# A four-image conv-attention and expert network on one core: the last attention block's sums move into its projection, and the end is re-ordered

## The chip, the cores and the metric

The kernel runs on one core of one Trainium2 chip, in one launch. The metric is the device time of that launch in microseconds (us). The core has a matrix engine (TensorE, "PE" in the profile; its weight loads are "PEld"), VectorE ("DVE"), ScalarE ("ACT"), GpSimd ("POOL") and SyncE ("SP"), which here only issues transfers. Sixteen DMA engines move data between HBM and the on-chip memory SBUF. TensorE writes to a second on-chip memory, PSUM, from which VectorE and ScalarE read.

## The reference: what is computed

The input x has 4 images of 128 channels and 64 x 64 = 4096 positions. Two layers follow each other, all in float32.

```python
# layer 0, per image (gn: group norm over groups of 4 channels)
e1, e2, asm = prelu(w1 @ gn(x)), prelu(w2 @ gn(x)), prelu(wa @ gn(x))   # 64, 64, 128 channels
x = x + softmax(e1.T @ e2) @ asm            # 4096 x 4096 scores
# layer 1, tokens t = x.T, per image (ln: layer norm over the 128 channels)
t = t + softmax((ln(t) @ Wq.T) @ (ln(t) @ Wk.T).T / 128) @ (ln(t) @ Wv.T)
logits = ln(t) @ gate_w.T + gate_b          # 64 experts
probs  = softmax(logits, axis=tokens)       # each expert picks its 8 best tokens
pooled = sum over those 8 of prob * ln(t)   # one vector for each image and expert
out_e  = gelu([pooled, 1] @ weight1[e]) -> [h, 1] @ weight2[e]   # 129x512, 513x128
t[token] += out_e * prob                    # given back to the 8 tokens
```

The two attentions are nearly all of the arithmetic. The experts are nearly all of the weights: 64 experts of 0.5 MB.

## The kernel before, in words

**Attention stages.** `stage(b, layer, ...)` runs the attention of one image and layer, in eight blocks n of 512 queries. `attention` (L523) makes the scores of four 128-key chunks at a time (L542, two PSUM tiles `ps`), ScalarE takes the exponential (L551), and `products` (L458) adds the product with the values into the PSUM tile `av`. The eight stages follow each other (L1082 to L1092); norms, projections and routing of other images are generators that are stepped beside them. The order within each engine is the order in which the Python code emits instructions, except where a scheduler moves one; `keep_in_program_order` pins an instruction, and `no_sync_barrier` lets no instruction move across it.

**Seven products.** In layer 1 the value product is a 2 x 2 block scheme with seven products instead of eight. `mix` (L483) makes the needed differences of two exponential tiles on VectorE, `mixed_products` (L495) adds seven products into the four quarters of `av[:, 0:2, 0:512]` (two halves of 64 partitions, two PSUM banks, two halves of 256 queries). The quarters have still to be added up to get the block's 128 x 512 result. `finish_attn` (L615) does that: ScalarE copies `av` to `c0`, `c1` and the half-swapped `sw` (L626 to L630), VectorE makes the sums `u` with six additions (L633 to L638). Then `u` is multiplied by `wvd`, the value weights with a 129th column that gives the softmax denominator (L647, `pv`); a reciprocal, a multiply-add with the residual `xq` and a copy of the denominator follow (L653 to L660).

**The last block.** For image 3, block 7 (`final`), no attention stage follows, so this chain is exposed: `xT` -> layer norm `norm_tokens` (L336; the power is taken on POOL, L181) -> transposes (`x_c` for the residual, stored to `x2` by ACT at L670; `l` at L678) -> `tg` -> gate product `pg` (L710) -> `M` -> `last_route` (L868): best eight, exponentials, the selection `zl` (L916), its transposes `pzT` (L923), `pool` (L928, L932) -> `pooledT`.

**Experts.** 16 groups g of 4 experts: `first_product` (L1124, `ph`, copied to `hp` by VectorE), `hidden` (L1134: transposes `pht`, bias add `hT`, GELU), `second_product` (L1147, `po`), each one group behind the one before. A group's weights are 2 MB, loaded by SP in two 1 MB halves (`load`, L1039). Nine places hold them: groups 0 to 8 go to places 0 to 8, group g + 9 to the place of group g, its first half after g's first product and its second half after g's second product. Groups 2, 6, 7 come early; groups 0, 1 go into the keys' and values' tiles `t`, `tt` as the last stage lets them go, 3 to 5 into `ring` when the attention's pool is released (L1103), group 8 into `late_place`, where the routing's tiles (pool `blk`) were (L1110 to L1117).

**Scores and checks.** `last_scores` (L936) is stepped in the expert loop at g = 11 (`half_g + 3`): VectorE's MATCH_REPLACE over 64 x 4096 (its line is L768), and after the loop ScalarE's exponentials and POOL's subtractions. At the same g `watch` (L1699) reduces the recorded softmax sums on VectorE, multiplies with ones on TensorE (L1720) and stores a count; after everything, a branch takes a general kernel if a sum was out of bounds (L1725).

**The end.** `first_pair` (the probabilities of images 0 and 1) is loaded into place 7 (L1194); the residual `x2` of two images and half of the positions is loaded into each of the places 0 to 3, one DMA an image (L1203). Then, for each pair i and block n, TensorE spreads the expert outputs (L1217, `px`), VectorE adds them to `x2` (L1224) and after every second block ACT issues two stores of 0.5 MB (L1227). The DMAs of SP and ACT share eight semaphores in turn, in the order in which the built program has them: each waits for the DMA eight before it.

Of the kernel before, what the change touches and what calls it, by code (L numbers as in the profile page):

```python
# [9 lines left out]
F32 = mybir.dt.float32  # L10
# [16 lines left out]
def tile_unshifted(  # L27
# [56 lines left out]
    def dram_tile(shape, name):  # L84
        return dram.tile(shape, F32, tag=name, name=name)

    x2 = [dram_tile([P, S], f"x2_{b}") for b in range(B)]
    x2_block = [[dram_tile([P, BLK], f"xb_{b}_{n}") for n in range(NB)] for b in range(B)]  # L90
# [327 lines left out]
    wvd = const.tile([P, C + 1], F32, tag="wvd", name="wvd")  # L418

    def weights_qk():  # L420
        wT = []
        for nm, w in (("q", wqT), ("k", wkT)):
            pw = ms_tile(f"pw{nm}")
            nc.tensor.matmul(pw[:, :P], lhsT=w, rhs=unfold, start=True, stop=True)
            t = block_tile("te", f"w{nm}")[:, :P]
            nc.vector.tensor_copy(t, pw[:, :P])
            wT.append(t)
        yield
        pw = ms_tile("pwqk")
        nc.tensor.matmul(pw[:, :P], lhsT=wT[0], rhs=wT[1], start=True, stop=True)  # L430
        nc.vector.tensor_copy(wqk, pw[:, :P])
        yield
        pw = ms_tile("pwv")
        nc.tensor.matmul(pw[:, :P], lhsT=unfold, rhs=wv, start=True, stop=True)
        nc.vector.tensor_copy(wvd[:, :C], pw[:, :P])
        nc.vector.tensor_copy(wvd[:, C : C + 1], last[:, 0:1])
        yield

# [176 lines left out]
    def finish_attn(b, n):  # L615
# [5 lines left out]

        direct, final = b == B - 1 and n >= NB - 2, b == B - 1 and n == NB - 1
        if final:
            c0, b1 = av[:, 0, :], av[:, 1, :]
        else:
            nc.scalar.copy(c0, av[:, 0, :])  # L626
            nc.scalar.copy(c1, av[:, 1, :])
            b1 = c1
        nc.scalar.copy(sw[lo, :], av[hi, 1, :])
        nc.scalar.copy(sw[hi, :], av[lo, 1, :])  # L630
        one, two = slice(0, HB), slice(HB, BLK)

        nc.vector.tensor_add(c1, b1, sw)  # L633
        nc.vector.tensor_add(u[:, two], c1[:, one], c1[:, two])
        nc.vector.tensor_add(u[:, two], u[:, two], c0[:, one])
        nc.vector.tensor_add(u[:, one], c1[:, two], c0[:, two])
        nc.vector.tensor_add(u[hi, one], u[hi, one], c0[hi, one])
        nc.vector.tensor_add(u[hi, one], u[hi, one], sw[hi, one])  # L638
        yield
# [3 lines left out]
        for k, (s0, ns) in enumerate(((2, 2), (0, 2)) if final else ((0, 3), (3, 1))):  # L643
            pv = ms_tile(f"pv{nm}_{k}")[:, : ns * (C + 1)].rearrange("p (s c) -> p s c", c=C + 1)
            for s in range(ns):
                for h in range(2):
                    nc.tensor.matmul(  # L647
                        pv[bass.ts(h, HC), s, :],
                        lhsT=u[:, (s0 + s) * P + h * HC : (s0 + s) * P + (h + 1) * HC], rhs=wvd,
                        start=True, stop=True,  # L650
                    )
            i = slice((b * NB + n) * SUB + s0, (b * NB + n) * SUB + s0 + ns)
            nc.vector.reciprocal(top_inv[:, i], pv[:, :, C])  # L653
            for s in range(ns):
# [4 lines left out]
                )  # L659
            nc.vector.tensor_copy(top_sum[:, i], pv[:, :, C])  # L660
        yield
        tb = pools["blk"].tile([P, SUB, C], F32, tag="tb", name=f"tb{nm}")
        tg = block_tile("c1", f"tg{nm}")
        if direct:
# [4 lines left out]
            to_channels(xT, xp, f"x2_{b}_{n}")  # L669
            nc.scalar.dma_start(out=x2[b][:, bass.ts(n, BLK)], in_=xp)  # L670
            yield
            if final:
# [68 lines left out]

    def small_tile(tag, b, width, dtype=F32):
        return small.tile([P, width], dtype, tag=tag, name=f"{tag}{b}")

# [93 lines left out]
    def early_route(b):  # L838
# [3 lines left out]
        m = M[b // 2][hs, : S - BLK]  # L842
        top, neg = small_tile("e_top", b, 8), small_tile("e_neg", b, 1)
        at, tot = small_tile("r_at", b, 8, mybir.dt.uint32), small_tile("e_tot", b, NB)
# [120 lines left out]


    def run(gen):
        for _ in gen:
            pass
# [69 lines left out]
    def load(g, i, h):  # L1039
        W[g] = places_of[i]  # L1040
        nc.sync.dma_start(out=W[g][:, h, :], in_=packed[g][:, h, :])
# [3 lines left out]
    def first_weights():  # L1045

        w1b = block_tile("xq", "w1b", 4)[:E, :]
        nc.sync.dma_start(out=w1b, in_=a["weight1"][:, D1 - 1, :])
# [20 lines left out]
    def last_weights(n, g):  # L1069
# [4 lines left out]
        if n == NB - 1:  # L1074
# [18 lines left out]
          ahead=mix_values(3), pace=(2, 1), hook=last_weights)  # L1093
    products()


# [8 lines left out]
    for g in range(3, 6):  # L1105
        new_place(g, ring, "w")
        for h in range(2):
            load(g, g, h)
    last_top = last_route(B - 1, pooledT)
    ends["blk"].close()  # L1110
    late = ctx.enter_context(tc.tile_pool(name="late", bufs=1, side="right", reuse_waits="tile"))
    late_place = late.tile([P, S], F32, tag="z", name="late_place")
    place(8, late_place)
    scores = last_scores(B - 1, *last_top)

    for h in range(2):
# [59 lines left out]
    for g in range(E // EG + 2):  # L1176
# [7 lines left out]
        for half, now in ((0, g), (1, g - 2)):  # L1184
            if 0 <= now and now + 9 < E // EG:
                load(now + 9, now, half)
        if g == half_g + 3:
            next(scores)
            watch(ms_tile("watch")[0:1, 0:1])
    next(scores)  # L1190
# [7 lines left out]
    for i in range(B // 2):  # L1198
        for q in range(2):
            ys.append(places_of[2 * i + q])  # L1200
            for h in range(2):
                tc.keep_in_program_order(
                    nc.sync.dma_start(out=ys[-1][:, h, :], in_=x2[2 * i + h][:, bass.ts(q, HS)])  # L1203
                )
    for i in range(B // 2):
        pe = ms_tile(f"poe{i}")
# [473 lines left out]
def tile_conv_attn_hybrid(ctx: ExitStack, tc: tile.TileContext, a: dict, out: bass.AP):  # L1680
# [17 lines left out]

    def watch(pc):  # L1699
        ok = guard.tile([P, 4], F32, tag="ok", name="ok")  # L1700

        later = tc.keep_in_program_order
        later(nc.vector.tensor_reduce(ok[:, 0:1], all_sum, axis=AX.X, op=ALU.max))
        later(nc.vector.tensor_reduce(ok[:, 1:2], all_inv, axis=AX.X, op=ALU.max))
        nc.vector.tensor_scalar(ok[:, 0:1], ok[:, 0:1], SAFE_SUM, None, op0=ALU.is_le)
        nc.vector.tensor_scalar(ok[:, 1:2], ok[:, 1:2], SAFE_INV, None, op0=ALU.is_le)
        later(nc.vector.tensor_reduce(ok[:, 2:3], top_sum, axis=AX.X, op=ALU.max))
        later(nc.vector.tensor_reduce(ok[:, 3:4], top_inv, axis=AX.X, op=ALU.max))
        nc.vector.tensor_mul(ok[:, 2:3], ok[:, 2:3], ok[:, 3:4])
        nc.vector.tensor_scalar(ok[:, 2:3], ok[:, 2:3], SAFE_RATIO, None, op0=ALU.is_le)  # L1710

        later(nc.vector.tensor_reduce(ok[:, 3:4], top_inv, axis=AX.X, op=ALU.add))
        nc.vector.tensor_scalar(ok[:, 3:4], ok[:, 3:4], SAFE_INV, None, op0=ALU.is_le)
        both = guard.tile([P, 1], F32, tag="both", name="both")
        nc.vector.tensor_mul(both, ok[:, 0:1], ok[:, 1:2])
        nc.vector.tensor_mul(both, both, ok[:, 2:3])
        nc.vector.tensor_mul(both, both, ok[:, 3:4])
        ones = guard.tile([P, 1], F32, tag="ones_g", name="ones_g")
        nc.gpsimd.memset(ones, 1.0)
        nc.tensor.matmul(pc, lhsT=both, rhs=ones, start=True, stop=True)  # L1720
        nc.vector.tensor_copy(count, pc)

# [44 lines left out]
```

## Time and profile before

| what | us |
|---|---|
| median of 3 runs | 3296.14 (3294.93 to 3297.43) |
| the profiled execution | 3298.76 |
| its span in the profile | 3297.0 |
| TensorE busy in the span | 3227.0 (98%) |
| VectorE busy | 2123.0 (64%) |
| ScalarE busy | 1253.4 (38%) |
| GpSimd busy | 424.4 (13%) |
| last value product of the attention ends | 3179.2 |
| first expert product starts | 3202.5 |
| first addition of the end (L1224) starts | 3264.4 |
| last addition of the end starts | 3285.5 |

All times in the profile are counted from the start of its span. The profiled execution is 2.62 us above the median of the runs, and 1.76 us of it lie outside the span. "Busy" for TensorE means that a product was in the pipeline; "granted clock" is the share of TensorE's full clock that it was given. A line such as `PE L542 ... ps<-q,t 128*64 128x512 f32 x4096` names engine, source line, output and input tiles, shape and count; a float32 product is recorded as two instructions. In a line of the timeline, the brackets hold the idle time of the engine before the instruction and what ended it. `w`, `t` and `tt` are names of tiles in the places above; `x` on the right of a DMA is an `x2` tensor, `wp` the packed weights.

### The profile page before, as it was taken

The page shows a single profiled execution, that of the slowest core. Times are in us where ns is not written, and L with a number is a line of the kernel's source. Part 1 is how long each engine was busy: PE and PEld are TensorE (multiplying, and loading weights), DVE is VectorE, ACT ScalarE, POOL GpSimd, SP SyncE. Part 2 cuts the span into 40 slices and gives each one's busy share as a digit, 9 for nine tenths or more (in the row PEclk, how much of TensorE's full clock was granted, in tenths as well). Part 3 has the DMA queues.
Part 4 walks back from the last instruction along what each step waited for, and adds up shares of the span by engine and source line. Part 5 has one row for each costly group of instructions (what it writes and reads, how often), then busy time and mean ns, then how long its engine had stood idle before and what let it go on. Part 6 is the DMA issues. An engine that isn't in the chain of part 4 may idle for free.

```text
span 3297.0 us, 49453 instructions
## 1 busy us (share of the span) xinstructions
PE 3227.0 (98%) x19764; PEld 1602.7 (49%) x19764; DVE 2123.0 (64%) x4192; ACT 1253.4 (38%) x1432; POOL 424.4 (13%) x414
## 2 busy tenths in 40 slices
PE   8999999999999999999999999999999999999986
PEld 4444444445555644444555554444444455454443
DVE  6665567556665667756675657765776566666566
ACT  2333334433333335333433335333333333343432
POOL 0111112310000004241000002242100002010011
PEclk9999999999999999999999999999999999999988
DMA  3221244223323222311120111321231010131059
GB/s 88 52 53 28 56 113 122 74 82 80 90 73 85 55 55 54 70 31 36 39 53 23 39 26 39 91 64 26 45 75 39 20 40 20 33 108 39 17 203 373
DMA packets 364753, 223.31 MB, mean 68 GB/s; under 512 B 273632, under 2 KB 298720, under 8 KB 359136
## 3 DMA queue, kind: packets, MB, share of 16 engines
q1 hardware_dynamic: 359056, 208.54, 23.6%
q10 hardware_dynamic: 4944, 10.46, 0.8%
q8 instruction: 157, 2.57, 0.3%
q0 software_dynamic: 512, 1.05, 0.1%
q14 instruction: 84, 0.69, 0.1%
HBM read 159.75 MB, written 97.19 MB: 78 GB/s over the span
## 4 chain that ended last, share of the span: by engine, by line
PE 96%; DVE 2%; DMA 1%; issue 0%; POOL 0%; ACT 0%; SPq 0%; ACTq 0%; DVEq 0%; POOLq 0%
PE ps L542 40%; PE av L476 27%; PE av L504 23%; PE pe L272 1%; PE pa L291 1%; PE pq L445 1%; PE pv L647 1%; PE ph L1127 1%; PE pg L710 0%; PE po L1157 0%; PE pd L590 0%; PE pht L1137 0%; DMA w<-x 0%; DVE tt L490 0%; DMA first_x<-in_x_dram 0%
## 5 line engine op out<-in xcount | busy, mean ns | idle before, releaser
L551 ACT ACTIVATE pt<-ps 128x1024 f32<-128x1024 f32 x1024 | 1021.7, 1024 | 1520.0 <-PE ps L542 1452.7
L542 PE MATMUL ps<-q,t 128*64 128x512 f32 x4096 | 929.3, 593 | 0.0
L476 PE MATMUL av<-pt,asm 64*128 64x512 f32 x4096 | 922.2, 589 | 0.9 <-ACT sw L630 0.9
L566 DVE TENSOR_TENSOR sacc<-sacc,pt 128x1024 f32<-128x1024 f32 x448 | 586.0, 1308 | 290.6 <-ACT pt L551 265.8
L504 PE MATMUL av<-pt,tt 128*64 128x256 f32 x3072 | 637.6, 379 | 0.0
L476 PEld LDWEIGHTS av<-pt,asm 64*128 64x128 f32 x4096 | 395.8, 187 | 485.5 <-issue 470.1
L490 DVE TENSOR_TENSOR tt<-pt 128x512 f32<-128x512 f32 x512 | 356.7, 697 | 372.6 <-ACT pt L551 355.9
L542 PEld LDWEIGHTS ps<-q,t 128*64 128x64 f32 x4096 | 315.8, 137 | 469.4 <-issue 442.1
L504 PE MATMUL av<-tt,mixed 128*64 128x256 f32 x2048 | 526.9, 380 | 5.4 <-DVE tt L490 5.4
L542 PE MATMUL ps<-e,e 64*128 64x512 f32 x2048 | 491.5, 597 | 2.1 <-DMA e<-ye 2.1
L504 PEld LDWEIGHTS av<-pt,tt 128*64 128x64 f32 x3072 | 359.9, 137 | 261.8 <-issue 137.9
L504 PE MATMUL av<-pt,mixed 128*64 128x256 f32 x1024 | 305.5, 380 | 0.0
L504 PE MATMUL av<-tt,tt 128*64 128x256 f32 x1024 | 305.2, 380 | 0.0
L542 PEld LDWEIGHTS ps<-e,e 64*128 64x128 f32 x2048 | 193.0, 187 | 230.5 <-issue 226.6
L504 PEld LDWEIGHTS av<-tt,mixed 128*64 128x64 f32 x2048 | 280.8, 137 | 8.6 <-DVE tt L490 6.3
L181 POOL TENSOR_TENSOR l_y<-l_v,mhalf 128x4 f32<-128x4 f32 x64 | 64.9, 1014 | 1586.8 <-DVE l_v L180 1586.5
L492 DVE TENSOR_TENSOR tt<-pt 128x256 f32<-128x256 f32 x512 | 220.5, 431 | 16.5
L491 DVE TENSOR_TENSOR pt<-tt,pt 128x256 f32<-128x256 f32 x512 | 218.6, 427 | 16.2
L504 PEld LDWEIGHTS av<-pt,mixed 128*64 128x64 f32 x1024 | 140.3, 137 | 61.3 <-DVE pt L491 0.3
L504 PEld LDWEIGHTS av<-tt,tt 128*64 128x64 f32 x1024 | 140.5, 137 | 1.9 <-DVE tt L492 0.7
L585 POOL TENSOR_TENSOR all_sum<-all_sum,c 128x512 f32<-128x512 f32 x32 | 44.0, 1375 | 522.2 <-DVE c L584 522.2
L182 DVE TENSOR_TENSOR l_z<-l_y 128x4 f32<-128x4 f32 x64 | 11.7, 183 | 97.0 <-POOL l_y L181 97.0
(248 smaller groups left out, 1779.3 us busy)
## 6 DMA issues: line engine op xcount, KB each, us to landing
wp<-in_weight_dram SPq DMA_DIRECT2D x128, 256.0 KB
w<-wp SPq DMA_DIRECT2D x22, 1024.0 KB
xq<-in_x_dram SPq DMA_DIRECT2D x32, 256.0 KB
rb<-inv SPq DMA_DIRECT2D x32, 256.0 KB
xT<-xt SPq DMA_DIRECT2D x128, 64.0 KB
ak<-xT SPq DMA_DIRECT2D x32, 256.0 KB
t<-kt SPq DMA_DIRECT2D x128, 64.0 KB
t<-t SPq DMA_DIRECT2D x32, 256.0 KB
```

The lines of the kernel that those rows point to most:

```text
L181: nc.gpsimd.tensor_tensor(y[:, :k], v[:, :k], mhalf[:, :k], op=ALU.pow)
L272: nc.tensor.matmul(pe[part, :], lhsT=w12[:, part], rhs=xn, start=True, stop=True)
L291: nc.tensor.matmul(pa[part, bass.ts(s, P)], lhsT=xn[:, bass.ts(s, P)][:, part], rhs=wa, start=True, stop=True,)
L476: nc.tensor.matmul(avs[b, 0, n][:, r, :], lhsT=values[b, 0][rows, j, :], rhs=pt[rows, h, :], start=(j == 0), stop=(j == NJ - 1),)
L490: nc.vector.tensor_sub(tt[:, 0:2, :], p4[:, :, 1, :], p4[:, 0, :, :])
L491: nc.vector.tensor_add(p4[:, 0, 1, :], tt[:, 1, :], p4[:, 0, 0, :])
L492: nc.vector.tensor_sub(tt[:, 2, :], p4[:, 1, 0, :], p4[:, 0, 1, :])
L504: nc.tensor.matmul(av[bass.ts(half, HC), bank, slot, :], lhsT=lhsT, rhs=rhs, start=first, stop=final, skip_group_check=True,)
L542: nc.tensor.matmul(ps[part, h, :], lhsT=key[:, part], rhs=q[rows, :], start=True, stop=True,)
L551: nc.scalar.activation(pt, ps, AF.Exp, scale=scale)
L566: nc.vector.tensor_add(sums[b, n], sums[b, n], pt)
L585: nc.gpsimd.tensor_add(all_sum, all_sum, c1)
```

## The change

It has five parts, nearly all at the end of the program.

- In the last block, VectorE no longer adds up the quarters. ScalarE copies `av[:, 1]` to `c1` and a quarter to `sw`, VectorE copies `av[:, 0]` to `c0` and another quarter to `sw`. Each 128-position chunk of the projection becomes three products that are added up in PSUM, with `wvd` and two new weight tiles: `wtwo` holds the lower half of `wvd` twice, `wsum` the sum of both halves twice. They are made once in `weights_qk`, in the first stage, by four copies on ScalarE and one addition on VectorE.
- `keep_busy(k, name)` emits k products of the identity with itself into a PSUM tile that nobody reads: 3 after the last value product, 3 after `pv`, 11 after the transposes `x_c`, 25 between `pg` and `pzT`.
- `watch` is split: the layer 0 part runs in the first step of `first_weights`, at the start of the last stage; the layer 1 part on VectorE directly before the expert loop; the product and the count copy in the loop. That and the MATCH_REPLACE come at g = 10 instead of 11.
- The two images of a pair of `x2` share one DRAM tensor, and the eight loads of 1 MB become four of 2 MB. A `no_sync_barrier` stands between them and the final loop. A place takes a merged load only when both halves of its weights have been used.
- Two small tiles of `early_route` get one buffer instead of two, and all parts of `watch` share one tile `ok`.

```diff
+    x2_pair = [dram_tile([2, P, S], f"x2_{i}") for i in range(B // 2)]
+    x2 = [x2_pair[b // 2][b % 2] for b in range(B)]
...
+        for half in (lo, hi):
+            nc.scalar.copy(wtwo[half, :], wvd[hi, :])
+            nc.scalar.copy(wsum[half, :], wvd[lo, :])
+        nc.vector.tensor_add(wsum, wsum, wtwo)
...
         if final:
-            c0, b1 = av[:, 0, :], av[:, 1, :]
+            nc.scalar.copy(c1, av[:, 1, :])
+            nc.vector.tensor_copy(c0, av[:, 0, :])
+            nc.scalar.copy(sw[lo, one], av[lo, 1, one])
+            nc.vector.tensor_copy(sw[hi, one], av[hi, 0, one])
...
-        nc.scalar.copy(sw[lo, :], av[hi, 1, :])
-        nc.scalar.copy(sw[hi, :], av[lo, 1, :])
-        nc.vector.tensor_add(c1, b1, sw)
-        nc.vector.tensor_add(u[:, two], c1[:, one], c1[:, two])
-        nc.vector.tensor_add(u[:, two], u[:, two], c0[:, one])
-        nc.vector.tensor_add(u[:, one], c1[:, two], c0[:, two])
-        nc.vector.tensor_add(u[hi, one], u[hi, one], c0[hi, one])
-        nc.vector.tensor_add(u[hi, one], u[hi, one], sw[hi, one])
...
+                if final:
+                    t = bass.ts(s, P)
+                    ts = slice(HB + s * P, HB + (s + 1) * P)
+                    parts = (
+                        ((c1[:, ts], wsum), (c1[:, t], wsum), (c0[:, t], wvd)) if s0
+                        else ((c1[:, ts], wsum), (c0[:, ts], wvd), (sw[:, t], wtwo))
+                    )
+                    for i, (lhsT, rhs) in enumerate(parts):
+                        nc.tensor.matmul(pv[:, s, :], lhsT=lhsT, rhs=rhs, start=(i == 0), stop=(i == 2))
+                    continue
...
+            if final:
+                keep_busy(FILL[1 + k], f"busy_b{k}")
...
+            if final:
+                keep_busy(FILL[3], "busy_c")
...
+    FILL = (3, 0, 3, 11, 25)
+    def keep_busy(k, name):
+        t = sc_tile(name)
+        for i in range(k):
+            tc.keep_in_program_order(
+                nc.tensor.matmul(t[:, i % 2, :P], lhsT=ident, rhs=ident, start=True, stop=True)
+            )
...
     def first_weights():
+        watch(0)
...
     products()
+    keep_busy(FILL[0], "busy_a")
...
+    keep_busy(FILL[4], "busy_d")
     last_top = last_route(B - 1, pooledT)
...
     scores = last_scores(B - 1, *last_top)
+    watch(1)
...
-        if g == half_g + 3:
+        if g == half_g + 2:
             next(scores)
-            watch(ms_tile("watch")[0:1, 0:1])
+            watch(1, ms_tile("watch")[0:1, 0:1])
...
-            for h in range(2):
-                tc.keep_in_program_order(
-                    nc.sync.dma_start(out=ys[-1][:, h, :], in_=x2[2 * i + h][:, bass.ts(q, HS)])
-                )
+            tc.keep_in_program_order(
+                nc.sync.dma_start(
+                    out=ys[-1],
+                    in_=x2_pair[i].rearrange("h c t -> c h t")[:, :, bass.ts(q, HS)],
 +                )
+            )
+    tc.no_sync_barrier()
```

The new `watch(0)` holds the two reductions over `all_sum` and `all_inv`, their two comparisons and a product; `watch(1)` holds the three reductions over `top_sum` and `top_inv` and five small operations, and with a PSUM argument only the product with ones and the copy to `count`.

## The prediction

> **What bounds the kernel now.** I read the page's slices first (part 2), then the chain of waits, then windows over the last 118 us. The slices say where to look:
>
> ```profile
> PE   8999999999999999999999999999999999999986
> ...
> PEclk9999999999999999999999999999999999999988
> DMA  3221244223323222311120111321231010131059
> GB/s 88 52 53 28 56 113 122 74 82 80 90 73 85 55 55 54 70 31 36 39 53 23 39 26 39 91 64 26 45 75 39 20 40 20 33 108 39 17 203 373
> ```
>
> TensorE is full in 37 slices, and the change touches none of its instructions there. In the last two slices it has holes, its clock falls, and the DMA share jumps to 5 and 9 tenths. The windows of that stretch (columns: engines' busy time and count, then granted clock, DMA share, GB/s):
>
> ```profile
> 3179.00:3182.00 3.00, 0.16 (x2) 0.00 (x0) 1.49 (x3) 1.16 (x2) 2.15 (x2) 0.97 0.60 142
> 3182.00:3199.00 17.00, 6.54 (x32) 3.88 (x32) 11.84 (x51) 3.32 (x8) 1.05 (x1) 0.50 1.01 419
> 3199.00:3210.00 11.00, 10.14 (x55) 4.76 (x57) 3.92 (x7) 2.31 (x4) 0.00 (x0) 0.69 0.87 296
> 3210.00:3264.00 54.00, 43.30 (x690) 26.85 (x684) 32.56 (x53) 17.31 (x23) 4.30 (x2) 0.90 1.01 419
> 3264.00:3268.00 4.00, 4.00 (x14) 1.15 (x10) 3.24 (x4) 1.78 (x2) 4.00 (x3) 0.60 0.32 125
> 3268.00:3273.00 5.00, 4.39 (x19) 1.20 (x16) 4.80 (x5) 0.00 (x0) 1.02 (x1) 1.00 0.98 386
> 3273.00:3278.00 5.00, 4.59 (x20) 1.20 (x16) 4.75 (x5) 0.00 (x0) 0.00 (x0) 1.00 0.95 249
> 3278.00:3293.00 15.00, 5.56 (x20) 1.20 (x16) 6.58 (x6) 0.00 (x0) 0.00 (x0) 0.71 1.02 414
> ```
>
> From 3182 on the 16 DMA engines are the bound: 419 GB/s wherever they have a queue. They fall short in two holes. Hole 1, 3199 to 3210: 11 x (1 - 296/419) = 3.2 us lost. Hole 2, 3264 to 3278: 4 x (1 - 125/419) + 5 x (1 - 386/419) + 5 x (1 - 249/419) = 2.8 + 0.4 + 2.0 = 5.2 us. Together 8.4 us. Who opens them is in SP's waits and in the end of the chain:
>
> ```profile
> SPq L1041 <- DVE halves L789: 16.1, 1, 16.1
> SPq L1203 <- DMA out_dram<-t: 13.8, 1, 13.8
> ```
> ```profile
> 3267.72 4.18 DMA out_dram<-t
> ...
> 3271.97 9.32 DMA w<-x
> ...
> 3281.40 1.23 DVE w L1224
> ```
>
> Hole 1: the seven loads issued from 3179.2 are through at 3199; the next, late_place's, wants the routing's tiles free (last halves, and zl read by pzT, which ends at 3199.28) and is issued at 3199.37. Hole 2: the last x2 load (1 MB) waits for an output store. In the built program each DMA of SP and ACT takes the next of eight semaphores and waits for its user eight DMAs earlier; two stores stand before this load in that order. So it is issued at 3271.97, while the stream had run dry at 3264.
>
> **The change part by part.** *(a) Last block's sums.* Before, in the timeline:
>
> ```profile
> 3180.44 0.69 DVE L633 TENSOR_TENSOR c<-av,sw 128x512 f32<-128x512 f32 x1 [4.61 <-ACT sw L630]
> ...
> 3185.25 0.17 DVE L653 RECIPROCAL top_inv<-pv 128x2 f32<-128x2 f32 x1 [0.52 <-PE pv L647]
> ```
>
> Removed: two ACT copies in series (0.58 + 0.58) and six VectorE adds (0.69, 0.54, 0.42, 0.41, 0.42, 0.42) between the last av (3179.16) and pv. Added: ACT copies 128x512 (0.59, row L627) beside a VectorE copy of 0.69 (row L1132) and two quarter-size copies (0.37 and 0.42) behind them. pv can start at 3179.95. Its work grows from 16 half-width products to 12 full ones. The nearest row is pa (L291, full width, 128 columns): 8 records in 1.16 us with a tail of 0.27, so 0.25 a product: 12 x 0.25 = 3.0, end 3183.0, second reciprocal at 3183.1 instead of 3185.25: **2.15 us earlier**, at full clock. At half clock (ph takes 1.94 there against 1.04, x 1.87) it is 5.7 us and nothing is won.
>
> *(b) Fills.* The clock fell 2.7 us after the last av and stood at 0.50 to 3205.7. Fills of 3, 3, 11 and 25 products x 0.25 take 0.8, 0.8, 2.8, 6.3 us; they lie in the waits for c1, xT, tb (3.1 us from x_c to l) and zl (6.0 us from pg's end to zl). The last has no room: it ends 0.3 to 0.4 us after zl. At full clock l gains 0.3, pg 0.5, pzT 0.3, pool 1.0 (1.97 + 0.63, about halved), the first two ph 1.4 (3.5 to 2.1). So zl comes 2.15 + 0.8 = 2.95 us earlier (3195.5), pzT ends at about 3196.4, first ph starts at 3198.8 (3202.5 before, 3.7 earlier), pht at 3201.1 (4.85 earlier).
> The Trainium skill (TensorE: Matmul & The Clock Gate, Part 1) gives a free-running window of 3.4 us, after which an idle array is halved; the fall at 3181.9 fits that. The same page (Part 4) says that transposes do not count as work, which speaks against x_c, l and pzT holding the clock; no row here shows transposes alone. The fills are plain products, so by that rule too only some 0.6 us a window is lost, and the sum stays.
>
> *(c) Checks.* The two reductions and three small operations of the first part (0.69 + 0.28 + 3 x 0.15 = 1.4 us, rows L1703 to L1706) go to the start of the last stage, where TensorE is full (50.00 of 50.00) and VectorE at 61%: nothing; uncovered, 1.4. The second part (1.4 us, 3240.4 to 3241.8) now lies on VectorE ahead of the first hp copy, which ph allows at 3199.9: 0 to 0.5 us, I take 0.3. What goes is the watch product's wait for it, 5.76 us of TensorE (3236.2 to 3241.95), and the half clock that follows (1.6 us). What is late next: the 4.42 us MATCH_REPLACE, one group earlier now, ahead of that group's hT and the next hp; the count copy behind it holds a PSUM tile that ph of group 12 needs. TensorE has 2.9 us of work there, so about 2 us of wait remain. Counting groups 10 to 15 at 2.54 us, the last po ends at about 3247, not 3257.2; the first x2 add moves from 3264.4 to about 3254.5.
>
> *(d) Loads.* Eight x2 loads become four of 2 MB, all ahead of every store, so none can wait for a store any more. Each now needs its group's second product where the first half needed only the first: at most group 12's, about 3240, when SP has nothing else queued and the engines still have first_pair to move (to about 3244). Hidden; if that cover went, 5 us (2 MB).
>
> *(e)* Four ACT copies and one add for wsum and wtwo in the first stage: under a full TensorE, nothing; at most 1.8 us by the rows of 0.37 and 0.42. SBUF addresses shift by some 1 KB: no row prices it; I take 0.
>
> **Sum.** After 3199 there are 11 x 296 + 54 x 419 + 4 x 125 + 5 x 386 + 5 x 249 + 15 x 414 = 35.8 MB to move. At 419 GB/s that is 85.4 us: 3199 to 3284.4, against 3293 now. VectorE's 16 adds (1.22 each, 19.8 us with gaps) from 3254.5 end at about 3278 even if the last load comes late, 6 us before the engines are through, so they do not decide. Gain: 3.2 + 5.2 = 8.4, less about 0.4 for slow starts that stay (385 GB/s at the first stores): **8.0 us**. The profiled execution took 3298.76 (span 3297.0), which becomes 3290.8; the runs shown have median 3296.14, 2.6 less, so 3288.1. No more than 8.6 can be had: the loads that begin at 3179.2 and their bytes stay.
> The Trainium skill (DMA: Bandwidth & Descriptors, Specifications) limits a core to about 358 GB/s from HBM; by that the 35.8 MB would take 100 us, more than the 94 measured with holes, so the trace (419 over 54 us) decides. The same table's fabric ceiling of 435 would end the stretch 3 us sooner; no window here reaches it.
>
> **Rivals.**
> 1. *Only the order of the loads counts.* If TensorE's chain does not get earlier (clock half in spite of the fills, or the MATCH_REPLACE costing what the watch cost), the stores still start at 3267.3, but the last MB flows at 3264 and nothing waits: 2.5 us of bytes out of the tail plus the 2.4 us of hole after 3268: 4.9 us, 3291.2. For it: (a) and (b) hang on the clock. Against: removing the watch wait alone moves the adds by over 5 us.
> 2. *Loads and stores hurt each other.* From 3273 to 3278 a load behind stores ran at 249 GB/s. If the roughly 3 MB of loads that will overlap with stores run so, 12.2 us instead of 7.3: gain 8.0 - 4.9 = 3.1, 3293.0. Against: at 3191 to 3195 ACT's 0.26 MB store ran amid loads, and the total stayed at 389 to 428 GB/s.
> 3. *Slower: the fills at half clock.* They stand in TensorE's order ahead of l and pzT. At x 1.87, 11 take 5.2 us and 25 take 11.8: l 2.7, pzT another 5.9 later, pv 0.6 later: pzT ends 9.2 us late, at 3208.5, and late_place's load is issued only then. The stream of 85.4 us and about 1 us of start then ends at 3294.9: 1.5 us late, 3297.7. It decides once pzT ends after about 3207. Against: continuous products raised the clock from 3202.5 to 3205.7, so the fills would warm it.
> 4. *The change does nothing that the end sees* (a hole reopens elsewhere as large): 3296.
>
> **How the numbers follow.** Forecast, 3286.5 to 3290: 0.60. Rival 1: 0.14. Rival 2: 0.11. Rival 4: 0.05. Rival 3: 0.05, three fifths of it with a worse price than worked out. Better than 3286.5, by scatter of the runs (1.3 us) or something I do not see: 0.05. A run can tell about 0.2% (6.6 us, 3289.5) from no change; of the forecast's share 0.03 lies on the near side of it. Faster 0.62, same 0.35, slower 0.03. The range takes in rival 1 and the near half of rival 2: 3285.8 to 3292.4.
>
> **What would show it.** Right: after 3182 a clock of 1.0 through pv, pg and pzT; the second top_inv reciprocal about 4 us after the last av, not 6; late_place's loads issued before the engines run dry; windows at 410 or more from there to the end; no x2 load waiting for a store; watch without wait, and about 2 us of wait behind the MATCH_REPLACE instead of 5.8. Wrong: a half clock in the fills, a window under 350 GB/s where loads and stores overlap, or the end set by the adds and not by the engines.

## The result, and the profile after

| | before | after |
|---|---|---|
| median, us (18 runs each) | 3296.69 | 3289.76 |
| lowest and highest run | 3294.03, 3299.56 | 3287.34, 3291.70 |
| the profiled execution | 3298.76 | 3289.95 |
| its span | 3297.0 | 3288.2 |
| last value product (av) ends | 3179.16 | 3177.25 |

The ratio is 0.9979, 95% interval 0.9972 to 0.9985: 6.93 us faster, by the interval 4.9 to 9.2, where 8.0 was forecast. In this study two executions ran at a lower granted clock, one of before (4892.13 us at 0.654) and one of the last kernel in the table below (3431.78 us at 0.944), and no median here counts them. The two profiled executions differ by 8.81 us, but 1.91 of it lies ahead of the change: the last av ends earlier. That is scatter of the attention stages. Over the 14 profiles of this study the last av ends anywhere from 3175.2 to 3179.2, and a kernel that has the attention of before unchanged (merged loads alone, below) had it at 3175.4. So times are compared from the end of the last av on, called T in what follows: from T to the end of the span it is 117.9 us before and 111.0 after, 6.9 us less.

The slices of the page of the changed kernel: the last two have a DMA share of 4 and 9 tenths at 186 and 392 GB/s, where they had 5 and 9 tenths at 203 and 373. Slices of 82 us are too coarse to show the holes; the windows behind them do.

```profile
DMA  3221244232323222311121111321131111131149
GB/s 88 52 54 27 58 112 122 74 82 77 94 71 87 55 55 52 67 37 36 39 46 30 37 29 39 87 68 26 40 80 30 30 37 23 26 114 30 27 186 392
```

The windows of the changed kernel over the same stretch (columns as before: engines' busy time, granted clock, DMA share, GB/s):

```profile
3179.00:3182.00 3.00, 2.87 (x26) 2.66 (x25) 2.48 (x12) 0.03 (x1) 0.45 (x2) 1.00 0.92 358
3182.00:3199.00 17.00, 15.46 (x114) 11.57 (x113) 10.76 (x47) 4.97 (x10) 1.04 (x1) 0.92 1.01 422
3199.00:3210.00 11.00, 11.00 (x150) 6.03 (x147) 5.64 (x9) 2.52 (x4) 0.00 (x0) 0.96 1.02 421
3210.00:3264.00 54.00, 43.97 (x596) 24.37 (x595) 35.76 (x43) 17.24 (x21) 9.31 (x4) 0.94 1.01 419
3264.00:3268.00 4.00, 3.59 (x16) 0.96 (x14) 3.77 (x4) 0.00 (x0) 0.00 (x0) 1.00 1.02 415
3268.00:3273.00 5.00, 4.56 (x18) 1.25 (x18) 4.72 (x5) 0.00 (x0) 0.00 (x0) 1.00 1.04 420
3273.00:3278.00 5.00, 1.03 (x4) 0.20 (x4) 2.33 (x2) 0.00 (x0) 0.00 (x0) 1.00 1.02 414
3278.00:3284.00 6.00, 0.00 (x0) 0.00 (x0) 0.00 (x0) 0.00 (x0) 0.00 (x0) 0.53 0.83 332
```

Both holes are gone: 421 GB/s where it was 296, and 415, 420, 414 where it was 125, 386, 249. What had opened them is in the timeline and the waits of the changed kernel: late_place's load is issued at 3194.28 (T + 17.0, before T + 20.2), the last x2 load at 3238.31 + 3.79 at the latest, more than 15 us ahead of the first store (3257.82), and the wait behind the MATCH_REPLACE is 2.2 us.

```profile
3180.99 0.17 DVE L678 RECIPROCAL top_inv<-pv 128x2 f32<-128x2 f32 x1
3194.28 0.79 SPq L1081 DMA_DIRECT2D late_place<-wp  x2
3238.31 3.79 SPq L1246 DMA_DIRECT2D w<-x  x2
```
```profile
PEld ph L1171 <- DVE count L1764: 2.2, 1, 2.2
```

The stream therefore ends some 8 us earlier after T, and yet the span ends only 6.9 us earlier. The last microseconds show the rest. Windows of 1 us at the end, first of the changed kernel, then of before:

```profile
3282.00:3283.00 1.00, 0.00 (x0) 0.00 (x0) 0.00 (x0) 0.00 (x0) 0.00 (x0) 0.50 0.65 266
3283.00:3284.00 1.00, 0.00 (x0) 0.00 (x0) 0.00 (x0) 0.00 (x0) 0.00 (x0) 0.50 0.24 90
3284.00:3285.00 1.00, 0.00 (x0) 0.00 (x0) 0.00 (x0) 0.00 (x0) 0.00 (x0) 0.50 0.11 25
```
```profile
3292.00:3293.00 1.00, 0.00 (x0) 0.00 (x0) 0.00 (x0) 0.00 (x0) 0.00 (x0) 0.50 0.95 381
3293.00:3294.00 1.00, 0.00 (x0) 0.00 (x0) 0.00 (x0) 0.00 (x0) 0.00 (x0) 0.50 0.28 107
3294.00:3295.00 1.00, 0.00 (x0) 0.00 (x0) 0.00 (x0) 0.00 (x0) 0.00 (x0) 0.50 0.10 41
```

Before, the share of the 16 engines falls from 0.95 to 0.28 within a microsecond: nearly all are through together. After, it decays from 3282: most engines are through, some are not. The DMA records of the trace say more: each engine closes its part of a store with a 4-byte record, though the record does not name the engine. For the last 16 such records, in us after T:

```
                 first  mean  last   last - mean   end of span - last
before           113.6  114.2 115.7  1.4           2.2
after            104.7  105.9 108.4  2.4           2.6
```

The mean comes 8.3 us earlier, which is what was forecast for the stream; the last engine only 7.3, and another 0.4 goes in what follows it: 8.3 - 1.0 - 0.4 = 6.9. The Trainium skill (DMA: Bandwidth & Descriptors, "Why a DMA increments its semaphore by 16 and not by 1") says that a DMA's engines finish independently and that only the full count means that all data has landed; these records agree. A few of the 16 records belong to the store before the last where an engine is late by more than one store; by the 16 counts on the last store's own semaphore the lags are 1.5 us before and 2.7 after, and the span ends 1.8 and 2.2 us behind the last count. These are single profiled executions, one of each kernel.

### The profile page after: what moved, and what is told of

Its sections match the earlier page's. It is cut to its first block, busy times and chain, and to the rows that moved or that the text cites. A ratio compares the mean times of both kernels' runs of the same rounds, so it can differ in the third digit from the quotient of the medians.

```text
span 3288.2 us, 49636 instructions
## 1 busy us (share of the span) xinstructions
PE 3230.3 (98%) x19856; PEld 1610.3 (49%) x19856; DVE 2118.7 (64%) x4189; ACT 1253.1 (38%) x1436; POOL 423.7 (13%) x414
## 4 chain that ended last, share of the span: by engine, by line
PE 96%; DVE 2%; DMA 0%; issue 0%; POOL 0%; ACT 0%; DVEq 0%; SPq 0%; ACTq 0%; POOLq 0%
PE ps L551 40%; PE av L485 27%; PE av L513 23%; PE pe L273 1%; PE pa L292 1%; PE pq L454 1%; PE pv L672 1%; PE ph L1171 0%; PE pg L739 0%; PE po L1201 0%; PE px L1265 0%; PE pd L599 0%; PE pht L1181 0%; DVE tt L499 0%; DVE w L1272 0%
```

## The experiments

The theory that I took into the experiments was that of the prediction: the end is bytes / 419 GB/s plus holes. Four runs that undo one part each, a fifth that makes one part alone, and a dose on TensorE should show which hole each part closes. All medians stand in one table. "Hole" is what the stream after T + 5 us lacks against 419 GB/s in the profiled execution, in us, from the bytes alone; "lag" is the last engine's record less the mean of the 16, as above; "gain" is the median of before, measured beside the run, less the median of the run. The medians of before lie between 3296.42 and 3296.94.

| run | median (runs) | gain | ratio to before, 95% | hole | mean, lag |
|---|---|---|---|---|---|
| changed kernel | 3289.76 (18) | 6.9 | 0.9972 to 0.9985 | 0.0 | 105.9, 2.4 |
| no fills | 3289.23 (11) | 7.7 | 0.9968 to 0.9986 | 0.8 | 106.7, 1.1 |
| old order of loads | 3289.85 (11) | 7.1 | 0.9970 to 0.9988 | 1.0 | 106.9, 1.7 |
| old checks | 3289.62 (11) | 7.3 | 0.9970 to 0.9988 | 1.9 | 107.7, 1.4 |
| old sums | 3289.69 (9) | 7.3 | 0.9967 to 0.9987 | 1.7 | 107.4, 0.7 |
| merged loads alone | 3292.52 (11) | 4.4 | 0.9979 to 0.9997 | 3.9 | 109.7, 1.6 |
| last fill of 60 | 3293.96 (11) | 2.9 | 0.9984 to 1.0002 | 5.7 | 111.5, 0.7 |
| ring first | 3285.92 (6) | 11.0 | 0.9956 to 0.9980 | 2.0 | 104.4, 0.6 |
| ring first, late_place free | 3286.68 (6) | 10.2 | 0.9956 to 0.9980 | 1.4 | 104.2, 1.6 |
| 24 rows of 8 KB | 3291.58 (11) | 5.0 | 0.9974 to 0.9992 | 0.0 | 106.6, 2.6 |
| 24 x 16 rows of 512 B | 3290.30 (11) | 6.2 | 0.9973 to 0.9991 | -0.1 | 106.4, 1.9 |
| old sums and old checks | 3290.91 (11) | 5.6 | 0.9975 to 0.9993 | 2.1 | 107.8, 1.0 |
| ring first, old sums | 3289.04 (11) | 7.4 | 0.9968 to 0.9986 | 3.4 | 106.2, 0.6 |

The intervals are some 6 to 8 us wide, so a difference of 1 or 2 us between two single rows is not settled by them; what follows rests on several rows together, or on runs that do not overlap.

**1. No fills.** 

```diff
-    FILL = (3, 0, 3, 11, 25)
+    FILL = (0, 0, 0, 0, 0)
```

> The changed kernel without its 42 filling products (FILL all 0). My theory (the 16 DMA engines set the end; TensorE counts only where it opens a hole in their stream): the clock falls some 2.7 us after the last av as it did before the change, zl comes about 0.8 us and pzT's end about 1.2 us later, so late_place's load is issued at about 18.2 us after the last av (17.0 with fills), still ahead of the point where the stream runs dry (19.8), but within the 1.8 us that an issue takes to its first bytes; the first ph products are slower by some 2 us and the loads behind them later: a hole of about 1 us, 0.5 to 1.5 us slower than the changed kernel (3290.3 to 3291.3). Rival 'TensorE's chain carries to the end': 3 us or more slower, 3292.8 or more. Rival 'the fills are worth nothing': within 0.3 us.

3289.23. The clock fell at T + 6.3 (T + 2.7 before the change) and stood at half until T + 23.4, and late_place's load was issued at T + 17.7 instead of 17.0. A hole of 0.8 us is there (the second of these two windows of the run, 395 GB/s); the time does not show it.

```profile
3182.00:3195.00 13.00, 3.66 (x14) 1.80 (x12) 8.44 (x36) 3.70 (x10) 1.05 (x1) 0.55 1.01 423
3195.00:3210.00 15.00, 14.57 (x159) 8.39 (x163) 7.48 (x18) 3.16 (x4) 0.00 (x0) 0.82 1.00 395
```

A clock of 0.55 over 13 us costs nothing here. The rival that TensorE's chain carries to the end is out.

**2. Old order of loads.** 

```diff
-                nc.sync.dma_start(out=ys[-1], in_=x2_pair[i]...[:, :, bass.ts(q, HS)])
-    tc.no_sync_barrier()
+            for h in range(2):
+                nc.sync.dma_start(out=ys[-1][:, h, :], in_=x2[2 * i + h][:, bass.ts(q, HS)])
```

> The changed kernel with the eight x2 loads of 1 MB in their old order, so that the last one again takes a semaphore that an output store holds. Theory: the first adds now come 7.5 us earlier after the last av than before the change, so the store that holds the semaphore is through at about 3262.5, the load is issued then and lands by about 3271, when the adds that need it are only just due (3272); stores flow meanwhile: 0 to 1.5 us slower than the changed kernel (3289.8 to 3291.3). Rival 'the order of the loads is most of the gain' (rival 1 of the prediction): 4 to 5 us slower, 3294 to 3295. In the trace: the wait of that load for out_dram<-t is back; theory: no window from 3255 to 3275 under 380 GB/s; rival: a window under 300.

3289.85, as the theory had it. Three views of this run, SP's waits, VectorE's timeline and the windows: the wait of SP for the store is back, and so are a wait of the adds for the last load and, against the expectation, a window under 380 GB/s:

```profile
SPq L1247 <- DMA out_dram<-t: 12.1, 1, 12.1
```
```profile
3271.82 3.70 DVE L1268 TENSOR_TENSOR w<-w,px 128x1024 f32<-128x1024 f32 x3 [1.71 <-DMA w<-x]
```
```profile
3266.00:3270.00 4.00, 3.56 (x14) 0.90 (x12) 3.87 (x4) 0.00 (x0) 0.00 (x0) 1.00 0.95 331
```

The last load goes at 3263.47 here, T + 86.6, where before it went at T + 92.8, because the stores begin 7.6 us earlier after T. The other parts had nearly closed hole 2 already.

**3. Old checks.** The two calls `watch(0)` and `watch(1)` and the old place of the scores go back (`half_g + 3`, all of `watch` behind them).

> The changed kernel with the old checks: all of them in one piece behind the scores of the last stage, and these one group later. Theory: TensorE waits 5.8 us for the watch product again, the last po ends and the first add starts about 4.7 us later (3259.6); the loads alone run dry at about 3262.6, the first store's bytes come at about 3264, and the adds then feed the stream at 423 GB/s, no faster than it drains, so the hole of 1.5 to 2.5 us stays: 3291.3 to 3292.3. Rival 'the adds had 6 us of slack, nothing': within 0.5 us. Rival 'the chain carries in full': 4.7 us slower, 3294.5.

3289.62. The first add came 4.3 us later (T + 82.0 instead of 77.7), the watch wait is back (the run's waits), and the stream has its hole of 1.9 us where the stores begin (its windows):

```profile
PE watch L1766 <- DVE both L1763: 5.8, 1, 5.8
```
```profile
3262.00:3280.00 18.00, 15.96 (x54) 4.16 (x50) 16.58 (x14) 0.00 (x0) 1.98 (x1) 0.92 0.96 379
```

The mechanism was as expected, and the cost was not there: here the theory first failed.

**4. Old sums.** The six additions and the 16 half-width products of the last block go back, the fills stay.

> The changed kernel with the old sums for the last block (two ACT copies in series and six VectorE adds ahead of pv, 16 half-width products), all else kept. Theory: the second top_inv reciprocal comes 2.3 us later, with it pzT and the issue of late_place's load, at 19.3 us after the last av; first bytes 21.1, the stream runs dry at 19.8: a hole of 1.3 us, 1 to 2 us slower than the changed kernel (3290.8 to 3291.8). Rival 'it lies beside the stream, nothing': within 0.5 us. Rival 'the chain carries in full, and the clock falls in the longer gap': 3 us or more.

3289.69. late_place's load is issued at T + 20.1, as late as before the change, the hole is 1.7 us (window of the run), and the time is the same.

```profile
3195.00:3210.00 15.00, 13.82 (x153) 8.50 (x152) 9.34 (x28) 4.26 (x6) 0.00 (x0) 1.00 0.93 375
```

Together the four runs have holes of 1.3 us in the mean, and medians that average 3289.60 against 3289.76. So holes of this size are free here.

**5. Merged loads alone**, in the kernel before.

> The kernel before with the loads part alone (four x2 loads of 2 MB, all recorded ahead of every store). Rival 1 of the prediction priced this at 4.9 us faster than before (3291.8 where before is 3296.7), and by the theory that the DMA engines set the end it should be so: the last MB flows at 3264 and the 2.4 us of hole behind it close, while hole 1 (3.2 us) and the late start of the stores stay. If loads and stores hurt each other (rival 2), the gain is 1 us or less.

3292.52, 4.4 us faster than before, with 4.9 expected. Hole 1 is left (351 GB/s over 15 us), and a smaller one at the stores (386), in the windows of the run:

```profile
3195.00:3210.00 15.00, 14.13 (x134) 7.83 (x133) 5.85 (x11) 3.54 (x5) 0.00 (x0) 0.79 0.93 351
3262.00:3280.00 18.00, 15.80 (x56) 3.91 (x52) 17.06 (x15) 0.00 (x0) 2.83 (x2) 0.98 0.97 386
```

So this part alone brings about two thirds of the gain, and the changed kernel without it loses nothing: the parts stand in for one another.

**6. A last fill of 60 products** (`FILL = (3, 0, 3, 11, 60)`).

> The changed kernel with 60 products instead of 25 in the last fill: 35 more at 0.234 us, 8.2 us of TensorE ahead of pzT. Theory: pzT's end and the issue of late_place's load come 8.2 less 0.3 (the slack of the fill) later; the load had about 0.9 us in hand against the dry point, so the stream stands empty for about 7 us: 6.5 to 7.5 us slower than the changed kernel, 3296.3 to 3297.3 (this is rival 3 of the prediction, by other means). Rival 'a queue of loads covers it, the adds have 6 us in hand': 2 us slower or less.

3293.96: 4.2 us slower than the changed kernel, not 6.5 to 7.5. late_place's load went at T + 24.2, 7.2 us later, and the stream was empty for 5.7 us, of which this window of the run shows most:

```profile
3199.00:3205.00 6.00, 5.13 (x47) 3.69 (x46) 1.74 (x10) 1.66 (x2) 0.00 (x0) 1.00 0.41 142
```

The hole was smaller than worked out (the load had 1.5 us in hand, not 0.9), and again some 1.5 us of it cost nothing. This is rival 3 of the prediction made to happen, and its price per microsecond.

**7. Ring first.** One load moved on SP's queue:

```diff
-    load(1, 1, 1)
     for g in range(3, 6):
         new_place(g, ring, "w")
         for h in range(2):
             load(g, g, h)
+        if g == 3:
+            load(1, 1, 1)
```

> The changed kernel with one load moved on SP's queue: the second half of group 1, which waits for the last av, is issued behind the two loads of group 3, whose place is free once the last but one group of av is done, some 3 us earlier. Theory (end = bytes / 419 GB/s from the first load on, plus holes): the stream starts about 3 us earlier and so runs dry 3 us earlier, at 16.9 us after the last av, but late_place's load is still issued at 17.0 and needs 1.8 us more: hole 1 opens again by about 2 us. Net 0.5 to 1.3 us faster than the changed kernel (3288.5 to 3289.3). Rival 'not the bytes but TensorE's chain and the adds set the end': within 0.3 us, and no hole matters.

3285.92, 3.8 us faster than the changed kernel; its six runs (3284.50 to 3286.58) do not overlap with the 18 of the changed kernel (from 3287.34). Group 3's loads go 4.3 us ahead of T (T is 3175.18 here), so that the stream gains 3.4 us: 1.8 us in the first five after T, and 0.7 MB (1.6 us) moved ahead of T. The hole ahead of late_place is there too, as expected. SP's timeline and the window of that hole:

```profile
3170.92 0.80 SPq L1081 DMA_DIRECT2D w<-wp  x2
...
3192.22 0.79 SPq L1081 DMA_DIRECT2D late_place<-wp  x2
```
```profile
3192.00:3195.00 3.00, 2.23 (x18) 1.65 (x22) 1.30 (x9) 1.59 (x2) 0.00 (x0) 0.91 0.65 161
```

By the old theory 3.4 - 2.0 = 1.4 us should be left. It is 3.8 by the medians and 3.4 from T on in the profiled executions: the hole cost nothing. This is the version to keep; it beats both kernels.

**8. Ring first, and late_place free early** (`got`, `exps` and `zl` in the buffers `inv`, `tb` and `sw`).

> As the one before, and the routing's tiles got, exps and zl are put in other buffers, so that late_place's 16 KB a partition are free once pg has read its tile: its load can be issued some 6 to 7 us earlier (about 10.5 us after the last av instead of 17.0). Theory: the stream starts 3 us earlier and does not run dry before the loads that follow the first ph products (issued 20.7 us after the last av); a hole of 0.6 to 1.5 us stays there: 1.2 to 2.6 us faster than the changed kernel (3287.2 to 3288.6). Rival 'the end is set elsewhere': within 0.3 us.

3286.68, no better than the one before. The load went at T + 10.3 and hole 1 closed, but a hole of some 1.4 us opened behind it, where the next loads wait for the first expert products.

**The theory formed in its place.** I call it S: the end is set by the slowest of the 16 DMA engines, not by their sum. They share every transfer equally, but an engine that is held up falls behind and stays behind as long as its queue is never empty. In a hole it catches up, because the others have nothing to do. The last column of the table speaks for it: the three kernels without a hole have lags of 2.4, 2.6 and 1.9 us, the other ten and before 0.6 to 1.7, 1.1 in the mean. The column says no more than this: the mean is the hole in other words (some 105.8 us plus the hole, wherever the bytes after T + 5 are the same), so a lag that shrinks as the hole grows means that the last engine did not come later.

The catching-up itself stands in the traces, in the 16 semaphore counts of each 1 MB load. Around hole 1, in us after T:

```
                               first of the 16   last three
before, last load ahead        20.0              20.7 20.7 22.0
before, first load behind      24.7              25.0 25.0 25.1
changed kernel, same stretch   20.2              20.7 21.8 22.0
changed kernel, next load      22.7              23.2 24.3 24.5
```

In the seven kernels in which hole 1 is over 1.5 us (before among them) the last count lies 1.2 to 2.0 us behind the median ahead of the hole and 0.2 to 0.4 behind it; in the three kernels without a hole it stays at 1.3 to 1.6. But this is not yet the lag of the last store: with old sums the last count is 1.6 us behind again at T + 30, and at T + 82 it is 1.6 behind there and 0.8 in the changed kernel. That hole 1 is what made the last lag small is therefore argued and not shown. Three runs try S further.

**9. and 10. Rows for one engine, and the control.** 24 stores from GpSimd behind late_place's load, in one run a row of 8 KB each, in the other 16 rows of 512 B:

```diff
+    for i in range(24):
+        spare = dram_tile([1, E * PAD], f"spare_{i}")
+        nc.gpsimd.dma_start(out=spare, in_=pooledT[0:1].rearrange("p e b -> p (e b)"))
```

> The changed kernel with 24 extra stores of one row of 8 KB (pooledT's partition 0, to spare DRAM) on GpSimd's queue behind the first products' input: 0.2 MB of transfers more. Four runs that each opened a hole of 0.8 to 1.9 us in the stream cost nothing. New theory S (the slowest of the 16 DMA engines sets the end, not their sum: the receipts of the last store come from 104.7 to 108.4 us after the last av, so one engine lags the mean by 2.5 us, and a hole shorter than that lag does not touch it): if a one-row transfer goes to one engine, that engine gets 24 x 0.31 = 7.4 us more work, and the end comes 4 to 7.5 us later (3294 to 3297). Old theory (end = bytes / 419 GB/s plus holes): 0.2 MB / 419 GB/s = 0.5 us (3290.3). If the row is spread over the engines, both say 0.5.

> The same 24 stores and the same 0.2 MB, but each as 16 rows of 512 B on 16 partitions: the control of the one before. Theory S and the old theory alike: if the rows are shared out over the engines, 0.5 to 1 us (3290.3 to 3290.8). If GpSimd's issuing or the number of stores is what costs in the one before, this one is as late as that.

3291.58 and 3290.30. It was no test: the trace has 384 data packets of 512 B in both, so the row was cut in 16. The Trainium skill (the section named above) says that a contiguous row can be split so that it goes to all 16 engines, and the records agree. The two runs move the same packets, so the 1.3 us between their medians (their runs lie between 3288.7 and 3292.2 in both) show how much a single median is worth here. What they do give is two more kernels without a hole and with a large lag.

**11. Old sums and old checks together.**

> The changed kernel with the old sums and the old checks together (fills and merged loads kept). Each of the two alone opened a hole (1.5 us ahead of late_place's load, 1.9 us ahead of the stores) and cost nothing. Theory S (some 1.5 to 2.5 us of hole are free, since the slowest engine catches up in them): both holes together are 3.5 to 4 us, so 1.5 to 2.5 us slower than the changed kernel (3291.3 to 3292.3). Rival 'holes cost in full, the four runs were scatter': 3.5 to 4 us (3293.3 to 3293.8). Rival 'sums and checks do nothing for the end, whatever the holes': within 0.5 us.

3290.91, 1.2 us slower than the changed kernel. The two holes do not add: with late_place's load late, the loads end later and the stores find less of a gap, so the hole is 2.1 us and not 3.5 to 4. The result lies between what S and the rival "nothing" give for 2.1 us (0.1 to 0.6, and 0) and the full price, and is inconclusive.

**12. Ring first with the old sums.** 

> The run with group 3's loads moved forward on SP's queue (3285.9), but with the old sums of the last block: late_place's load is issued about 3 us later (20.1 instead of 17.0 us after the last av), while the stream runs dry at 16.9, so the hole ahead of it grows from 2.1 to about 5 us. Theory S (the slowest DMA engine sets the end; only what a hole has over some 1.5 to 2 us of lag costs): the first 2 us were free, the next 3 are not: 2.5 to 3.5 us slower than that run, 3288.4 to 3289.4. Rival 'the sums do nothing for the end', which fits the run with the old sums in the changed kernel (3289.7 against 3289.8): 3285.3 to 3286.6. Rival 'only the first microseconds of the stream count': the same.

3289.04, 3.1 us slower than ring first; its lowest run (3286.77) lies above that run's highest. Nothing else differs than the sums, which in run 4 were worth nothing. late_place's load went at T + 19.0 and the hole is 3.4 us in all, in this window of the run:

```profile
3192.00:3199.00 7.00, 5.81 (x50) 3.82 (x52) 4.88 (x18) 2.00 (x3) 0.00 (x0) 1.00 0.56 194
```

The expected 2.5 to 3.5 was met by the median, but with a hole that grew by 1.4 us and not by 3: neither S nor the old theory gives 3.1 us for that. The two profiled executions differ by 2.1 us from T on, and their last engine by 1.8. So part of the agreement is luck, and some 1 to 2 us of the difference stay unexplained. Both figures say that a part that is free beside one dry point is not free beside an earlier one. The rival "the sums do nothing for the end" is out.

## Why the prediction was right, point by point

- **The bound.** Right: 419 GB/s wherever there is a queue (422, 421, 419, 415, 420, 414 in the windows), and ring first shows it from the other side: a stream that begins 3.4 us earlier ends the program 3.8 us earlier.
- **(a) Sums.** Right in size: second reciprocal 2.34 us earlier (T + 3.75), with 2.15 forecast. The four copies did not run beside each other: in the built program each waits for the other engine's, and the timeline has them in series from 3177.32 to 3179.49. The products that need them last hide it.
- **(b) Fills.** Right in what they do: clock 1.00 from 3180 to 3196, first ph 4.45 us earlier (T + 18.9), 3.7 forecast. The last fill ended 0.2 us ahead of zl instead of after it (0.234 us a product, not 0.25). What was not foreseen is that the clock fell again behind them, to 0.57 from 3196 to 3200, so the first two ph took 3.5 us, as before, and not 2.1. Run 1 shows that the end sees none of this. One reading was too strong: the fall at 3181.9 came 2.7 us after the last product, less than the 3.41 us in which the clock's record steps, so the stretch that ended there was not idle throughout.
- **(c) Checks.** Mechanism right, one term too small: the wait behind the MATCH_REPLACE is 2.2 us (about 2), the second part costs ph and hp nothing (0.3 was taken). But groups 13 to 15 take 3.43 us each and not 2.54, since three `pht` in a row wait 0.81 us for their hp (one did before); the first add comes 7.5 us earlier after T, not 9.9. It had 6 us in hand, so this cost nothing.
- **(d) Loads.** Right: hidden, and none waits for a store. Alone it brings 4.4 us where rival 1 gave 4.9. With the other parts it is not needed (run 2), which the prediction did not say.
- **(e).** Nothing seen, as forecast; no run tries it alone.
- **The sum.** This is the step that was off: "35.8 MB at 419 GB/s ... 3199 to 3284.4". The holes closed in full, and the mean engine was through 8.3 us earlier. Taking the end to follow the mean put the gain 1.1 us too high: the last engine now lags by 2.4 us instead of 1.4, and 0.4 went behind it. The median of 3289.76 lies only 0.24 us inside the forecast's upper end of 3290, less than medians scatter here (run 9 and 10), so that it fell inside is partly luck. And the pricing of single parts failed: fills, sums, checks and the order of loads are each worth nothing when undone alone (runs 1 to 4), though each opens a hole again.
- **The rivals.** 2 did not happen: loads and stores together ran at 414 to 420. 3 did not, and run 6 shows that its price would have been about 4 us for a delay of 7. 1 described one part rightly. That S is the reason for the free 1.5 us is argued: it fits runs 1 to 8 within their scatter, 9 and 10 were no test, run 11 leaves it open, and run 12 costs more than it gives. That the last engine to finish sets the end is what the records say (in all 14 profiles the span ends 2.2 to 2.9 us after the last record, and 1.8 to 2.2 after the last count on the last store's semaphore). What makes an engine lag is shown in part only, see below.

## What to carry to other kernels

When DMA engines are the bound, count each hole in their stream, and do not expect the whole sum: here some 1.5 us of it were free, since the end follows the slowest engine, and a hole lets it catch up. Parts of a change that close the same hole cannot be priced one by one; a part that is worth nothing today (the sums, in run 4) can be worth 2 to 3 us once the stream starts earlier (run 12). The first question is then not how to fill the holes but which load can be queued sooner: one moved line brought more than half of what the whole change did.

## What was not expected of the hardware

- **DMA engines drift apart under a full queue.** In the changed kernel the records of the 1 MB loads come every 2.47 us, 14 engines together and two 1.2 us behind; after an instruction fetch of 16 KB at T + 25.2, which held one engine for 1.09 us, a third one is 1.2 us behind in the loads that follow. The next four fetches, at T + 35.1, 42.1, 49.6 and 63.3, each add one more: four, five, six and seven late counts. There are ten such fetches after T (0.95 to 1.09 us each) and ten of 8 KB (0.3 to 0.4). The Trainium skill (Runtime: NRT & Kernel Launch, "Instruction fetch mechanics") says that an engine refills its instructions in blocks of 16 KiB over a DMA queue and that this is mostly hidden. The trace agrees on the size for these ten; whether the fetching engine waits was not looked at, but the loads that share the DMA engine are held up, as the third laggard shows. The first two laggards do not each answer to a fetch, so other causes remain open.
- **The clock falls although TensorE works.** The last fill ended at 3193.21; `pzT` (0.43 us of transposes) and `pool` (1.5 us of products of 64 columns) followed, and from 3196 the granted clock was 0.57 for 4 us, with TensorE busy 3.84 of 4.00. No run tells whether the transposes, the narrow products or the gaps of 0.3 to 0.5 us between them did it. They are not enough by themselves: in runs 9 and 10 the same chain kept a clock of 1.00 there, and the first two ph took 1.9 us instead of 3.5. In the clock's record of all 14 profiles every stretch at half speed after T, except the last one, which is cut off by the end, lasts 3.41 us or a whole multiple of it, so where such a step falls may decide; this is a guess.
- **A single row of 8 KB is cut in 16.** 24 such stores left 384 packets of 512 B, the same as 16 rows of 512 B each.
